# Sorted chunks of a graph layer with 424 edges and one scatter, scatters that wait for picking, and another order within a step

## The chip, the cores and the metric

The kernel runs as one program on one core of a Trainium2 chip. The metric is the device time of one execution in microseconds (us). The engines are named as the profile names them: PE is TensorE (PEld are its weight loads), DVE is VectorE, ACT is ScalarE, POOL is GpSimd and SP is SyncE. Lines such as L947 are lines of the kernel before; the lines of the changed kernel differ.

## The reference, cut to what matters

A message-passing layer over 412,500 edges that are sorted by `dst`, with 12,500 nodes of 128 features:

```python
h = jnp.maximum(_layernorm(x, axis=-1), 0.0)
# of the layer, with idx_i = src (not sorted) and idx_j = dst (sorted):
h = h @ W_in2f
Wij = ssp(f_ij @ W_f1 + b_f1) @ W_f2 + b_f2     # ssp(x) = softplus(x) - log 2; f_ij: 20 numbers an edge
Wij = Wij * rcut_ij[:, None]
x_ij = h[idx_j] * Wij                           # the message of an edge
agg = jax.ops.segment_sum(x_ij, idx_i, num_segments=N)
out = ssp(agg @ W_o1 + b_o1) @ W_o2 + b_o2
x = x + out
```

Two parts are irregular: `h[idx_j]` is read by an index that is sorted, and the messages are summed by an index that is not.

## The kernel before

Edges are taken in chunks of 512 (four tiles of 128), four chunks are a group, and there are 204 groups, of which 814 chunks hold edges. `step(k)` writes out one step of a software pipeline in which every engine does its share for another chunk; the order of the calls in it is the order of the instructions on each engine, since the schedule is written by hand. In step k:

- `rows` (SP, six chunks ahead) loads the 32 rows of `h` that a chunk can need into `near`; they are kept as three bfloat16 parts. `window` (DVE) makes `at`, which marks the row of each edge, and `pick` (PE, two chunks ahead) multiplies the two, which gives `h[idx_j]` for each edge in `ps`. `picked` (ACT) scales it by `rcut_ij`.
- `hidden` (PE), `exp` and `log` (ACT) make ssp(f W_f1 + b) for two chunks at a time in the one bank `z`; `value` (PE, one chunk ahead) multiplies it by W_f2 onto the bias that `bias` (ACT) has put into `v`.
- `message` (DVE) multiplies the two into `o`, a buffer of two chunks; there are four such buffers.
- Then POOL scatters `o` into a table in DRAM, one indirect DMA for each tile of 128 edges: edge by edge to `slot`, a row that belongs to the node block (128 nodes) of its `src`. The table is written through 16 views (`VIEWS`), which the kernel declares to be disjoint, in turn. A scatter waits until the scatter that last used its semaphore (eight before) or its view has landed.
- `blocks`, `rank` and `rank_end` (DVE and PE) find `slot`: a running count for each of the 98 node blocks is kept in one bank of PSUM, `free`, and `top` is read from it.

A segment (`SEGS`, eight runs of groups) has a table of its own. After a segment its table is read back and summed by node: `load` (SP) brings tiles of 128 slots (`m`), `compare` (DVE) marks the node of each slot (`to`), `add` (PE) multiplies the two into `acc`, a tile being one matmul of two passes, and `keep` (DVE) adds four blocks to `agg`. A planner spreads these units over the later steps; from the sizes of the segments it gives 6.08 tiles a step from step 245, and 8.86 from step 629 to the end of the edges. The last segment's 206 tiles come after the last scatter, with the output layers between them.

In 32 groups (`SORTED`, from group 6 to 150, four or five groups apart) the edges of a chunk are first sorted by node block. `Permute` does it on the chip, 19 to 4 steps ahead; its `move` multiplies the edges' data by marks into `z` and `moved` (ACT) copies `z` to `ev`. A chunk then has only 480 edges (`PV` of each 128), laid out so that 256 (`FIXED`) stand at fixed places. Those tiles are stored by a plain DMA into `fix` (the list `statics`, issued in the next step), and only the other two tiles of the chunk need a scatter. `ev` holds the marks in its last 32 partitions, so `Permuted.pick` takes three matmuls of 32 rows for each tile, one for each part of `h`.

Of the kernel before, what the change touches and what calls it, by code (L numbers as in the profile page):

```python
# [23 lines left out]
SEGS = (59,39,30,27,19,14,8,8)  # L24
RW = P + 1
VIEWS = 16
# [11 lines left out]
PV = 120  # L38
# [3 lines left out]
FIXED = 2 * P  # L42
# [23 lines left out]
def gnn_kernel(  # L66
# [31 lines left out]
    assert D == P and src_n.shape == (P, NT) and NW <= P  # L98
# [14 lines left out]
    class Segment:  # L113
# [4 lines left out]
        def __init__(self, k):  # L118
# [10 lines left out]
            self.kw = NW if here and here[-1] == permuted[-1] else 0  # L129
# [19 lines left out]
            self.rows = self.row(NBLK)  # L149
            self.all = self.rows + self.nw * FIXED  # L150
# [25 lines left out]
        def row(self, b):  # L176
            return (b * self.T + min(max(b - self.b0, 0), self.b1 - self.b0)) * P
# [57 lines left out]
    fix = tc.dram_tile([NW * FIXED, RW], F32, name="fix")  # L235
# [138 lines left out]
    def permute_constants():  # L374
# [29 lines left out]
        for T in sels:  # L404
            edge_t = T * P
            half_t = edge_t / 2
            for t, (e0, e1, c) in enumerate(((1.0, 0.0, -edge_t), (0.5, 0.5, -half_t - 1.0),
                                             (0.5, 0.5, -half_t), (0.0, 1.0, -1.0))):
                turn_t = -1.0 if t % 2 else 1.0
                nc.vector.memset(lifts[T][:, t:t + 1], c - BIG * turn_t)  # L410
# [251 lines left out]
    with tc.tile_pool(name="edge", bufs=2) as edge, tc.tile_pool(  # L662
# [47 lines left out]

        class Group:


            def __init__(self, g):
# [30 lines left out]
                self.near = {}  # L745

            def rows(self, c):
# [8 lines left out]
                nc.sync.dma_start(self.near[c], h3_t[t][bass.ds(start, WR), :]  # L756
                                  .rearrange("r (k f) -> (r k) f", f=P))

            def columns(self):
                if len(self.cols) == 3:  # L760
# [24 lines left out]
                    nc.vector.tensor_copy(start_t[:, :, 0], row_t[:, 0, :, 0])  # L785
                    nc.vector.tensor_add(start_t[:, :, 1:3], row_t[:, 0, :, 1:3],
                                         row_t[:, 1, :, 1:3])
                    for t, half in ((1, -1.0), (2, 0.0)):
                        nc.vector.tensor_scalar(start_t[:, :, t], start_t[:, :, t], 0.5,
                                                seg.T * P / 2 + half, op0=ALU.mult, op1=ALU.add)  # L790
                    nc.vector.tensor_scalar(start_t[:, :, 3], row_t[:, 1, :, 3],
                                            seg.T * P - 1.0, None, op0=ALU.add)
# [55 lines left out]
            def rank_end(self, c):  # L848
# [63 lines left out]
            def value(self, c, v):  # L912

                r = self.pair[c // 2 * 2][:, c % 2, :]
                for i in range(QT):
                    nc.tensor.matmul(v[:, i, :], r[:, i * P:(i + 1) * P], wf2,  # L916
                                     start=False, stop=True, skip_group_check=True)
                return v

            def pick(self, c, at, ps):  # L920

                near = self.near.pop(c)
                for i in range(QT):
                    nc.tensor.matmul(ps[:, i, :], at[:, i * P:(i + 1) * P], near,  # L924
                                     start=i == 0, stop=i == QT - 1, skip_group_check=True)

# [9 lines left out]
            def message(self, c, v, hg):  # L936
# [6 lines left out]
                nc.vector.tensor_mul(o[:, :, :P], v, hg)  # L943
                views = self.seg.views
                for i in range(QT):
# [6 lines left out]
                    )  # L952
                    due = [self.seg.clears[w] for w, d in enumerate(self.seg.cleared)
# [14 lines left out]
        class Permuted(Group):  # L968


            def __init__(self, g):
                super().__init__(g)
                self.from_ = permutes[g]

            def rows(self, c):

                k = self.g * NCHUNK + c
                t = table_of[k]
                i = int(k >= FIRST)
                at = k - heads[i].start  # L980
                if c % 2 == 0:
                    self.near_p = quad_room().bitcast(BF16)
                self.near[c] = self.near_p[3 * WR:, c % 2 * 3 * P:(c % 2 + 1) * 3 * P]
                start = nc.sync.value_load(shifts[i][0:1, at:at + 1], min_val=0,
                                           max_val=tables[t][1] - WR)
                nc.sync.dma_start(self.near[c], h3_t[t][bass.ds(start, WR), :])
# [14 lines left out]
            def over(self, c, i):  # L1001

                s = self.from_.scalars.rearrange("p (w t) i -> p w t i", w=NCHUNK)
                return s[:, 2 * c:2 * c + 2, 0:2, i]

            def blocks(self, c):
                if c < NCHUNK - 1:
                    return
                for h in range(2):
                    blk = edge.tile([P, QT], F32, name="blk_p")  # L1010
                    nc.vector.tensor_scalar(blk.rearrange("p (w t) -> p w t", w=2),
                                            self.over(h, 2), -1.0, None, op0=ALU.add)
                    inb = quad.tile([P, QT, NBLK], F16, name="inb", bufs=4)
                    nc.vector.tensor_tensor(
                        inb, count_ps[:, None, :NBLK].to_broadcast([P, QT, NBLK]),
                        blk[:, :, None].to_broadcast([P, QT, NBLK]), op=ALU.is_equal)
                    self.inb[h] = inb.rearrange("p t b -> p (t b)")

            def rank(self, c):

                if c < 2:
                    return
                self.pass_on()
                kept["inb"] = self.inb[c - 2]
# [3 lines left out]
            def rank_end(self, c):  # L1028

                if c < 2:  # L1030
                    return
                h = c - 2
# [4 lines left out]
                top_w = top.rearrange("p (w t) -> p w t", w=2)  # L1037
                nc.vector.tensor_add(top_w, top_w, self.over(h, 3))
# [831 lines left out]
```

## Time and profile before

| | us |
|---|---|
| three runs | 3958.76, 3964.23, 3968.8 |
| median | 3964.23 |
| the profiled execution | 3958.62 |
| its span, first to last instruction | 3956.9 |

| engine | busy us | share of the span | instructions |
|---|---|---|---|
| PE | 3331.5 | 84% | 24536 |
| PEld | 2657.4 | 67% | 24536 |
| DVE | 3116.8 | 79% | 8634 |
| ACT | 2437.4 | 62% | 5637 |
| POOL | 2896.1 | 73% | 3018 |

TensorE's granted clock was 0.91 of full speed on average. In a group's row, the numbers after the bar are its busy time in us and the mean of one instruction in ns, and after the second bar the idle time of the engine just before them with what ended most of it; "issue" is time in which the profile shows nothing that the engine waited for. A row of waits has the total in us, the number of waits and the longest. In the timeline a row has the start, the length, and in brackets the idle time before it and its releaser.

### The profile page before, as it was taken

Reading aid. Unit: us, or ns where it says so; the run is one execution under the profiler, and the core shown is the slowest. Engines: PE = TensorE matmul, PEld = TensorE weight load, DVE = VectorE, ACT = ScalarE, POOL = GpSimd, SP = SyncE. Lnnn points to the kernel's source line nnn. Section 1 sums busy time; section 2 is a strip of 40 time slices with the busy share of each in tenths; the row PEclk is TensorE's granted clock in tenths of the full one; section 3 lists DMA queues with packets and bytes.
Section 4 is the critical chain, followed back from the end, with each engine's and each line's share of the span. In section 5 each row is a group of like instructions: output and inputs, shape, how many; then the busy total and the mean of one; then the engine's idle time right before and its main releaser. Section 6 shows DMA issues by size and latency. Waiting matters only on the chain. (4 is left out here: it accounts for less than half of the span.)

```text
span 3956.9 us, 80101 instructions
## 1 busy us (share of the span) xinstructions
PE 3331.5 (84%) x24536; PEld 2657.4 (67%) x24536; DVE 3116.8 (79%) x8634; ACT 2437.4 (62%) x5637; POOL 2896.1 (73%) x3018
## 2 busy tenths in 40 slices
PE   6777877777788988989989989888888889988968
PEld 4555555554467777777767767777676778777867
DVE  7978777766678888888888879788777778787867
ACT  5776677766666666666656656666555555554625
POOL 5777777777777777777777777777777777777760
PEclk9888788887899999999999999999889999999989
DMA  6787666665567878877777767887788779777766
GB/s 171 217 264 246 182 185 177 180 188 167 151 190 222 230 220 253 252 223 219 221 246 231 209 190 206 237 252 205 227 245 235 205 228 288 226 211 216 217 191 189
DMA packets 644371, 852.03 MB, mean 215 GB/s; under 512 B 240230, under 2 KB 442082, under 8 KB 643934
## 3 DMA queue, kind: packets, MB, share of 16 engines
q1 hardware_dynamic: 547502, 648.36, 59.3%
q0 software_dynamic: 96000, 198.34, 15.0%
q8 instruction: 198, 3.24, 0.4%
q14 instruction: 239, 1.96, 0.2%
q10 hardware_dynamic: 432, 0.13, 0.0%
HBM read 427.81 MB, written 418.61 MB: 214 GB/s over the span
## 5 line engine op out<-in xcount | busy, mean ns | idle before, releaser
L947 POOL DMA_INDIRECT slots<-o,slot x2744 | 2646.2, 964 | 868.2 <-issue 642.7
L1378 PEld LDWEIGHTS acc<-to,m 128*128 128x128 f32 x8464 | 1080.7, 205 | 398.2 <-DVE to L1362 171.7
L1378 PE MATMUL acc<-to,m 128*128 128x128 f32 x8464 | 1171.2, 294 | 189.7 <-DVE to L1362 99.2
L916 PEld LDWEIGHTS v<-wf,r 128*128 128x128 f32 x6512 | 916.2, 209 | 125.0 <-ACT v L909 58.6
L916 PE MATMUL v<-wf,r 128*128 128x128 f32 x6512 | 947.8, 293 | 33.2 <-ACT v L909 32.3
L809 ACT ACTIVATE r<-z,bf 128x1024 f32<-128x1024 f32 x407 | 451.7, 1110 | 629.1 <-PE z L801 524.2
L909 ACT ACTIVATE v<-bf 128x512 f32<-128x512 f32 x812 | 488.3, 601 | 545.5 <-DVE o L943 483.5
L932 ACT ACTIVATE hg<-picked,rcut 128x128 f32<-128x128 f32 x2744 | 775.1, 368 | 77.5 <-PE picked L924 77.1
L1362 DVE TENSOR_TENSOR to<-count_ps,m 128x640 f32<-128x640 f16 (+5 forms) x945 | 675.2, 741 | 57.2 <-DMA m<-slots 43.3
L943 DVE TENSOR_TENSOR o<-v,hg 128x512 f32<-128x512 f32 x686 | 468.9, 684 | 65.3 <-ACT hg L932 33.2
L814 ACT ACTIVATE r<-r,half 128x1024 f32<-128x1024 f32 x407 | 462.4, 1136 | 0.0
L924 PE MATMUL picked<-near,at 96*128 96x128 bf16 x2744 | 282.4, 228 | 187.1 <-DVE o L943 98.0
L849 DVE TENSOR_REDUCE top<-free 128x4 f32<-128x392 f32 x686 | 379.4, 553 | 71.3 <-PE free L844 70.4
L801 PE MATMUL z<-f,wf 20*128 20x512 f32 x1372 | 414.8, 682 | 0.0
L818 DVE TENSOR_TENSOR inb<-count_ps,blk 128x392 f16<-128x392 f16 x686 | 380.3, 555 | 38.0 <-PE count_ps L1213 26.1
L924 PEld LDWEIGHTS <-at 96*128 96x128 bf16 x2744 | 225.1, 103 | 220.3 <-issue 188.7
L877 PE MATMUL free<-inb,rest_of 128*128 128x392 f16 x750 | 266.2, 355 | 79.4 <-DVE top L849 77.8
L1087 POOL DMA_INDIRECT slots<-o,slot_p x256 | 247.2, 965 | 78.1 <-issue 47.3
L941 DVE COPY o<-place 128x8 f32<-128x8 f32 x343 | 64.7, 188 | 302.6 <-DMA slots<-o,slot 283.1
L844 PE MATMUL free<-inb,after 128*128 128x392 f16 x686 | 244.6, 356 | 8.6 <-DVE used L883 6.2
L896 DVE TENSOR_SCALAR at<-rel,prow 96x512 bf16<-96x512 bf16 x686 | 246.0, 359 | 0.0
L1074 ACT ACTIVATE hg<-picked,scalars 128x128 f32<-128x128 f32 x512 | 144.4, 367 | 8.5 <-PE picked L1063 8.5
(228 smaller groups left out, 2853.8 us busy)
## 6 DMA issues: line engine op xcount, KB each, us to landing
m<-slots SPq DMA_DIRECT2D x200, 387.0 KB
rel<-rel_d SPq DMA_DIRECT2D x172, 384.0 KB
m<-slots SPq DMA_DIRECT2D x198, 322.5 KB
m<-slots SPq DMA_DIRECT2D x227, 258.0 KB
slots<-zero SPq DMA_DIRECT2D x106, 516.0 KB
m<-slots SPq DMA_DIRECT2D x98, 451.5 KB
slots<-o,slot POOLq DMA_INDIRECT x2744
f<-in_f_n SPq DMA_DIRECT2D x408, 80.0 KB
```

The source lines that it names most:

```text
L801: nc.tensor.matmul(z[:, k, :], wf1[rows, :], self.f[rows, :], start=True, stop=True)
L809: nc.scalar.activation(r, z, AF.Exp, bias=bf1, accum_out=exps[:, i:i + 1])
L814: nc.scalar.activation(r, r, AF.Ln, bias=half, scale=0.5)
L818: nc.vector.tensor_tensor(inb, count_ps[:, None, :NBLK].to_broadcast([P, QT, NBLK]), self.blk[:, c * QT:(c + 1) * QT, None].to_broadcast([ ...
L909: nc.scalar.activation(v, spread(bf2, QT), AF.Copy)
L916: nc.tensor.matmul(v[:, i, :], r[:, i * P:(i + 1) * P], wf2, start=False, stop=True, skip_group_check=True)
L924: nc.tensor.matmul(ps[:, i, :], at[:, i * P:(i + 1) * P], near, start=i == 0, stop=i == QT - 1, skip_group_check=True)
L932: nc.scalar.activation(hg[:, i, :], ps[:, i, :], AF.Copy, scale=self.rcut[:, j:j + 1])
L943: nc.vector.tensor_mul(o[:, :, :P], v, hg)
L947: put = nc.gpsimd.indirect_dma_start(out=views[j % VIEWS], out_offset=bass.IndirectOffsetOnAxis(ap=self.slot[:, j:j + 1], axis=0), in_=o[: ...
L1362: nc.vector.tensor_tensor(to[:p, a:e, :], count_ps[:p, None, :].to_broadcast([p, e - a, P]), self.m[u][:p, a:e, P:].to_broadcast([p, e - a ...
L1378: nc.tensor.matmul(self.acc[b // self.size][:, i, :], m[:p, j, :P], to[:p, j, :], start=t == 0, stop=t == self.seg.read(b) - 1)
```

## The change

Sorted chunks have 424 edges (`PV` 106), `FIXED` is three tiles of four, and the last tile is the only one that is scattered. The same 32 groups are sorted, so that there are three more plain groups: 207 groups, 828 chunks with edges. The four scattered tiles of a sorted group are ranked together, once. The marks of a sorted chunk are copied by DMA to 96 partitions and `near` is loaded in three parts, so that its pick is the plain one, four matmuls of 96 rows. There are seven segments; the planner now gives 4.52 tiles a step from step 257, 6.53 from 481 and 9.54 from 621. Slots are no longer clamped to the table: the start of every block is moved up by half a tile, and the bound on the count is folded into the instruction that turns it.

Within a step the scatters move out of `message` into `put`, behind the picking; `window` stands ahead of the picking; `exp`, the sorting's `moved` and `product` and the ranking follow it; `hidden`, `keep` and `add` come last. The first scatter of each chunk k also waits for the pick of chunk k+2 (`PACE`).

```diff
-SEGS = (59,39,30,27,19,14,8,8)
+SEGS = (62,56,35,24,14,8,8)
+PACE = {0: (("pick", 2),)}
...
-PV = 120
+PV = 106
...
-FIXED = 2 * P
+SETS = (32,)
+FIXED = 3 * P
...
-            self.rows = self.row(NBLK)
-            self.all = self.rows + self.nw * FIXED
+            self.rows = self.row(NBLK) + P // 2
+            self.all = self.rows + self.nw * P
...
+        behind_of = {}
+        def behind(put, name):
+            tc.add_manual_dep(put.ins, name,
+                              mybir.DependencyInfo(mybir.DependencyClass.Sync,
+                                                   mybir.DependencyReason.DATA),
+                              reason="order of scatters")
+        def paced(put, k, i, n):
+            for event, ahead in PACE.get(i, ()) if n > 1 or i else PACE.get(1, PACE.get(0, ())):
+                name = behind_of.get((event, min(k + ahead, NCH - 1)))
+                if name:
+                    behind(put, name)
...
-                    nc.vector.scalar_tensor_tensor(top, top, -BIG,
+                    nc.vector.scalar_tensor_tensor(top, top, BIG + (seg.T + 1) * P / 2 - 1.0,
                                                    turn.rearrange("p c t -> p (c t)")[:, w],
-                                                   op0=ALU.add, op1=ALU.mult)
-                    nc.vector.tensor_add(top, top, self.start[:, w])
-                    nc.vector.tensor_scalar(self.slot[:, w], top, 0.0, float(seg.rows - 1),
-                                            op0=ALU.max, op1=ALU.min)
+                                                   op0=ALU.min, op1=ALU.mult)
+                    nc.vector.tensor_add(self.slot[:, w], top, self.start[:, w])
...
         class Permuted(Group):
...
             def rows(self, c):
                 if c % 2 == 0:
-                    self.near_p = quad_room().bitcast(BF16)
+                    at = quad_room().bitcast(BF16).rearrange("p (w e) -> p w e", w=2)
+                    self.at_of[c // 2] = at
+                    for q in range(WP // WR):
+                        nc.sync.dma_start(at[q * WR:(q + 1) * WR], self.from_.ev[c // 2][WP:])
+                super().rows(c)
...
-            def pick(self, c, at, ps):
-                for i in range(QT):
-                    for q in range(3):
-                        nc.tensor.matmul(ps[:, i, :], at[:, i * P:(i + 1) * P],
-                                         near[:, q * P:(q + 1) * P],
...
-                for i in range(2):
-                    j = c % 2 * 2 + i
-                    nc.gpsimd.indirect_dma_start(
-                        out=self.seg.views[(c * QT + i) % VIEWS],
...
+            def put(self, c):
+                o = self.out.pop(c)
+                put = nc.gpsimd.indirect_dma_start(
+                    out=self.seg.views[c * QT % VIEWS],
+                    out_offset=bass.IndirectOffsetOnAxis(ap=self.slots[:, c:c + 1], axis=0),
+                    in_=o[:, 0, :],
+                    in_offset=None,
+                )
+                paced(put, self.g * NCHUNK + c, 0, 1)
...
         def step(k, units=(), aside=()):
...
-            sorting(k, "moved")
             part("log", min(k + LZ - 2, made["exp"]), pairs(hidden_log))
-            part("exp", min(k + LZ - 1, made["hidden"]), pairs(hidden_exp))
             if has(k):
                 g.message(c, vs.pop(k), hgs.pop(k))
...
+            part("window", k + 3, window)
...
                 g.pick(c, ats.pop(k + 2), ps[k + 2])
...
-            part("window", k + 3, window)
+            if has(k):
+                g, c = of(k)
+                g.put(c)
             for c, u in units:
                 c.compare(u)
                 compared.append((c, u))
-            for c in owed:
-                c.keep()
-            owed.clear()
+            part("exp", min(k + LZ - 1, made["hidden"]), pairs(hidden_exp))
+            sorting(k, "moved")
+            sorting(k, "product")
             if not aside:
                 sorting(k, "taken")
-            part("hidden", k + LZ, pairs(hidden))
-            sorting(k, "product")
-            for c, u in compared:
-                c.add(u)
-            compared.clear()
...
             sorting(k, "ready")
+            part("hidden", k + LZ, pairs(hidden))
             for c, u in units:
                 c.load(u + AHEAD)
+            for c in owed:
+                c.keep()
+            owed.clear()
+            for c, u in compared:
+                c.add(u)
+            compared.clear()
```

What moved shows on three engines. First GpSimd, where a sorted group meets the plain group behind it; `slot_p` marks the scatters of sorted chunks, and the names in brackets are the semaphores that a scatter waits for (DMASW0 to 7 are those of the eight scatters before it). Before:

```order
L1087 DMA slots_118<-o,slot_p 141824x129 [waits DMASW4_49,DVE_49]
L1087 DMA slots_118<-o,slot_p 141824x129 [waits DMASW5_49]
L1087 DMA slots_118<-o,slot_p 141824x129 [waits DMASW6_49,DVE_49]
L1087 DMA slots_118<-o,slot_p 141824x129 [waits DMASW7_49]
L947 DMA slots_118<-o,slot 141824x129 [waits DMASW0_49,DVE_49]
L947 DMA slots_118<-o,slot 141824x129 [waits DMASW1_49]
```

And after the change:

```order
L1106 DMA slots_118<-o,slot_p 136320x129 [waits DMASW4_49,DVE_49,PE_49]
L1106 DMA slots_118<-o,slot_p 136320x129 [waits DMASW5_49,DVE_49,PE_49]
L1106 DMA slots_118<-o,slot_p 136320x129 [waits DMASW6_49,DVE_49,PE_49]
L1106 DMA slots_118<-o,slot_p 136320x129 [waits DMASW0_49,DMASW7_49,DVE_49,PE_49]
L983 DMA slots_118<-o,slot 136320x129 [waits DMASW4_49,DVE_49,PE_49]
L983 DMA slots_118<-o,slot 136320x129 [waits DMASW1_49]
```

The group has four scatters for eight, each with a wait for PE, and the first plain scatter behind it waits for DMASW4, the semaphore of the scatter four before it, instead of DMASW0.

Next TensorE, from the last picking matmul of one step to the value of the next (chunk 378 is picked; `free` is the ranking, `acc` the sums, `z` the hidden layer). Before:

```order
L924 MATMUL picked<-near,at 128x128
L801 MATMUL z<-f,wf_62 128x512 x2
L1378 MATMUL acc<-to,m 128x128 x10
L877 LDWEIGHTS rest_of
L877 MATMUL free<-inb,rest_of 128x392
L844 LDWEIGHTS after
L844 MATMUL free<-inb,after 128x392
L916 MATMUL v<-wf_63,r 128x128 x4
```

And after the change:

```order
L954 MATMUL picked<-near,at 128x128
L906 LDWEIGHTS rest_of
L906 MATMUL free<-inb,rest_of 128x392
L875 LDWEIGHTS after
L875 MATMUL free<-inb,after 128x392
L832 MATMUL z<-f,wf_62 128x512 x2
L1397 MATMUL acc<-to,m 128x128 x5
L945 MATMUL v<-wf_63,r 128x128 x4
```

The sums and the hidden layer moved behind the ranking, to the end of the step, and in this step one unit of sums stands where there were two.

Last ScalarE, near the same place (`hg` is picked, `v` the bias, `r,exps` the exp, `r<-r` the log, `xo<-z` the sorting's copy). Before:

```order
L909 ACTIVATE v<-bf_68 128x512
L809 ACTIVATE r,exps<-z,bf_66 128x1024
L932 ACTIVATE hg<-picked,rcut 128x128 x4
L909 ACTIVATE v<-bf_68 128x512
L1279 ACTIVATE xo<-z 128x1024
L814 ACTIVATE r<-r,half 128x1024
```

And after the change:

```order
L963 ACTIVATE hg<-picked,rcut 128x128 x4
L938 ACTIVATE v<-bf_68 128x512
L1298 ACTIVATE xo<-z 128x1024
L963 ACTIVATE hg<-picked,rcut 128x128 x4
L938 ACTIVATE v<-bf_68 128x512
L840 ACTIVATE r,exps<-z,bf_66 128x1024
```

The exp and the sorting's copy moved from the beginning of their steps to the end, behind the bias.

More of the change, by code (lines that the diff above doesn't have):

```diff
@@ L128, in __init__ @@
             self.here = here
-            self.kw = NW if here and here[-1] == permuted[-1] else 0
+            ended = [i for i in range(len(SETS)) if permuted[sum(SETS[:i + 1]) - 1] in here]
+            assert len(ended) < 2 and sum(SETS) == NPG
+            self.set = ended[0] if ended else None
+            self.kw = SETS[self.set] * NCHUNK if ended else 0
             plain = (self.c1 - self.c0 - self.nw) * CH
@@ L745, in __init__ @@
                 self.near = {}
+                self.out = {}
             def rows(self, c):
```

119 lines of the change are left out of this document (56 added, 63 removed).

## The prediction

> **What bounds the kernel now.** I read the page's first part, then its costliest groups, then busy time by stretch, because the engine with the most busy time (TensorE) is not the one that sets the end.
>
> ```profile
> span 3956.9 us, 80101 instructions
> L947 POOL DMA_INDIRECT slots<-o,slot x2744 | 2646.2, 964 | 868.2 <-issue 642.7
> L1087 POOL DMA_INDIRECT slots<-o,slot_p x256 | 247.2, 965 | 78.1 <-issue 47.3
> ```
>
> GpSimd looks 73% busy, but it does nothing except scatter, and before nearly every scatter stands a gap that nothing ends ("issue"). The next rows are GpSimd's timeline at the start and the end, and one line of the waits.
>
> ```profile
> 27.25 1.13 POOL L947 DMA_INDIRECT slots<-o,slot  x1 [23.71 <-DVE at L896]
> 39.70 0.96 POOL L947 DMA_INDIRECT slots<-o,slot  x1 [7.55 <-DVE at L896]
> 40.97 0.95 POOL L947 DMA_INDIRECT slots<-o,slot  x1 [0.30 <-issue]
> 3842.14 0.96 POOL L947 DMA_INDIRECT slots<-o,slot  x1 [0.30 <-issue]
> POOL slots L947 <- issue: 642.7, 2107, 0.3
> L947 POOLq EVENT_SEMAPHORE  x720: 17/17/2349, 39.5 to 3833.0; - x180
> ```
>
> A scatter is 0.964 us and its gap 0.30 us, so one takes 1.265 us of GpSimd, and a plain chunk (four) takes 5.06 us. Busy time by stretch (each row: the stretch and its length, then busy us and count of PE, PEld, DVE, ACT and POOL, TensorE's clock, DMA share, GB/s) shows that the queue never stops: the scatters come to 778, 798, 475 and 790, and 2841 x 1.265 = 3594 of the 3600 us from 200 to 3800.
>
> ```profile
> 200.00:1190.00 990.00, 755.89 (x4918) 527.48 (x4917) 733.40 (x2395) 680.15 (x1596) 752.99 (x778) 0.83 0.66 193
> 1190.00:2200.00 1010.00, 903.97 (x7205) 740.28 (x7205) 847.71 (x2321) 650.48 (x1504) 766.89 (x798) 0.96 0.80 231
> 2200.00:2800.00 600.00, 532.58 (x4147) 436.68 (x4144) 495.22 (x1291) 375.52 (x871) 455.44 (x475) 0.94 0.76 215
> 2800.00:3800.00 1000.00, 872.43 (x6560) 749.56 (x6559) 761.96 (x1784) 551.32 (x1292) 759.35 (x790) 0.92 0.79 228
> ```
>
> So GpSimd's scatter queue is the bound from 40 to 3843 us; 114 us of last sums and output follow. What the rest could do without it shows in the waits of VectorE for a free `o` (four buffers of two chunks, freed by landed scatters). These rows are, in turn, from the first, second, third and fourth of those stretches.
>
> ```profile
> DVE o L941 <- DMA slots<-o,slot: 89.8, 26, 8.6
> DVE o L1081 <- DMA slots<-o,slot: 49.8, 17, 7.2
> DVE o L941 <- DMA slots<-o,slot_p: 4.1, 1, 4.1
> ...
> DVE o L941 <- DMA slots<-o,slot: 35.1, 24, 4.4
> DVE o L1081 <- DMA slots<-o,slot: 33.1, 9, 8.6
> DVE o L941 <- DMA slots<-o,slot_p: 8.3, 5, 3.7
> ...
> DVE o L1081 <- DMA slots<-o,slot: 24.2, 6, 6.8
> DVE o L941 <- DMA slots<-o,slot: 15.9, 7, 5.7
> DVE o L941 <- DMA slots<-o,slot_p: 5.1, 2, 3.2
> ...
> DVE o L941 <- DMA slots<-o,slot: 138.3, 54, 6.4
> ```
>
> The messages (L943 and L1084, one a chunk) count the chunks in the same stretches:
>
> ```profile
> 200.00:1190.00 990.00, 116.85 (x171) 0.83 0.66 193
> 1190.00:2200.00 1010.00, 118.15 (x173) 0.96 0.80 231
> 2200.00:2800.00 600.00, 73.11 (x107) 0.94 0.76 215
> 2800.00:3800.00 1000.00, 136.13 (x199) 0.92 0.79 228
> ...
> 200.00:1190.00 990.00, 34.30 (x50) 0.83 0.66 193
> 1190.00:2200.00 1010.00, 34.23 (x50) 0.96 0.80 231
> 2200.00:2800.00 600.00, 16.43 (x24) 0.94 0.76 215
> ```
>
> That is 221, 223, 131 and 199 chunks; the stretches are cut near chunks 257, 481 and 612, where the change moves sums. Without the waits (143.7, 76.5, 45.2, 138.3 us) a chunk would take the other engines 3.83, 4.19, 4.24 and 4.33 us. This free pace is somewhat flattering, since they work ahead during a wait.
>
> **The scatters removed (the main term).** Plain chunks go from 686 to 700, sorted chunks stay 128 with one scatter for two: 2800 + 128 = 2928 scatters for 3000. 72 x 1.265 = -91.1 us of the queue that sets the end. It holds as long as the queue stays full. GpSimd's need for a chunk becomes (4 x plain + sorted) x 1.265 / chunks: 4.20, 4.21, 4.37 and, where nothing is sorted, 5.06 us. Against the free pace, 0.37, 0.02, 0.13 and 0.73 us a chunk are left over, so the second and third stretch need the smaller terms.
>
> **Sums.** 4164 tiles for 4232, but placed otherwise: the planner's rate from chunk 257 to 481 falls from 6.08 to 4.52 tiles a step, from 481 to 621 it rises to 6.53, after that from 8.86 to 9.54. The rows here are the sums (L1378) in the second stretch, and three groups that the next parts use.
>
> ```profile
> 1190.00:2200.00 1010.00, 370.03 (x2706) 341.89 (x2706) 0.96 0.80 231
> L924 PE MATMUL picked<-near,at 96*128 96x128 bf16 x2744 | 282.4, 228 | 187.1 <-DVE o L943 98.0 <-DVE o L1084 37.7 <-ACT hg L932 28.5
> L1063 PE MATMUL picked<-xo 32*128 32x128 bf16 x1536 | 110.5, 219 | 21.5 <-DVE o L943 9.6 <-DVE o L1084 5.5 <-ACT hg L932 2.8
> L809 ACT ACTIVATE r<-z,bf 128x1024 f32<-128x1024 f32 x407 | 451.7, 1110 | 629.1 <-PE z L801 524.2
> ```
>
> A pass of the sums takes 370.03 / 2706 = 0.137 us of TensorE, a tile two passes, 0.27 us. So TensorE gets 0.43 us a chunk lighter, then 0.12 and 0.19 us heavier.
>
> **Sorted chunks elsewhere.** Picking falls from twelve matmuls of 0.072 us to four of 0.103: -0.45 us a sorted chunk, -0.10 us on average. One ranking for two, and no clamp, make VectorE lighter too. None of this is on GpSimd's path, so it earns nothing by itself, but the free pace becomes 3.73 us (first), 3.66 (to chunk 481), 4.26 (to 612) and 4.52 (rest), against needs of 4.20, 4.21, 4.37 and 5.06. GpSimd stays last everywhere, by 0.11 us where it is closest. Fourteen more chunks cost ScalarE the most, whose 680 of 990 us have room. The stores of sorted rows grow by half (128 x 66 KB more) while less is cleared, at a DMA share of 0.66 to 0.80: 0.
>
> **SyncE.** Its issues go from 3630 to 3995: a sorted group issues twelve small loads of `near` and six copies of its marks where it issued four. A short issue was 0.37 us:
>
> ```profile
> 2026.11 0.37 SPq L1471 DMA_DIRECT2D fix<-o  x1
> 2008.47 0.95 POOL L947 DMA_INDIRECT slots<-o,slot  x1 [0.30 <-issue]
> 2011.36 0.17 DVE L1081 COPY o<-scalars 128x8 f32<-128x8 f32 x1 [1.00 <-DMA slots<-o,slot]
> 2018.57 0.96 POOL L947 DMA_INDIRECT slots<-o,slot  x1 [0.30 <-issue]
> 2025.29 0.18 DVE L1081 COPY o<-scalars 128x8 f32<-128x8 f32 x1 [8.58 <-DMA slots<-o,slot]
> ```
>
> 14 x 0.37 = 5.2 us within four steps of some 17 us, issued six steps ahead of the pick (L1469), which is the cover: 25 us. Zero; if the cover went, up to 5.2 us on each of 32 groups.
>
> **A new wait behind the sorted groups.** Slots are written through sixteen views in turn, and the sorted chunks now use views 0, 4, 8 and 12. In the new order the first scatter after a sorted group waits for the one four before it (view 0 again), where every scatter otherwise waits for the one eight before. Four scatters are 5.06 us. How long a scatter takes to land is told by the last four rows above. The scatter begun at 2008.47 is the last of the buffer that the copy at 2011.36 waited for, 2.9 us; from 2018.57 to 2025.29 it is 6.7 us. So a sorted group costs 0 to 1.7 us on GpSimd's own path, all later scatters standing behind it: 0 to 54 us over 32. I take 0.5 us: the middle of the two landings, 4.8 us, just passes without a wait, so about half of them would pay, up to 1.7 us: +16 us.
>
> **Scatters wait for picking.** Four scatters queue behind each such wait. Wherever VectorE waits for an `o`, GpSimd is some six chunks behind, so picking two chunks on is long past; and one more semaphore to look at is 17 ns (the row above), with the same 0.30 us gap in front of scatters that have one or none: 0, at most 828 x 0.017 = 14 us. At the start GpSimd is not behind; the first chunk's wait disappears in the 7.55 us that it idles anyway, the next few cost: +1 us (-1 to +6).
>
> **The step's new order.** Sums now stand last on TensorE, `exp` behind picking on ScalarE, and sorting's matmuls right behind the pick, needing the bank that `exp` frees. If TensorE waits there, it is for at most one such pass of ScalarE (L809, 1.1 us) at four steps of a sorted group, 4.4 us. The spare in a cycle (18.6 chunks, before chunk 481) is 8 us or more, so nothing; from 481 to 612 it is about 2.3 us, so up to 2.1 us on seven groups, 15 us. ScalarE idles a third of the time and should be ahead: +4 us (0 to 15). The tail works through 206 tiles as before: 0 (4 us either way).
>
> **Sum.** The profiled execution took 3958.6 us (span 3956.9), 5.6 below the median of 3964.2 and the least of the three. 3958.6 - 91.1 + 16 + 1 + 4 = 3888.5, call it 3888.
>
> **A rule weighed.** TensorE's clock was 0.83 in the first stretch at 76% busy and 0.96 in the second at 90%. A chunk took it 903.97 / 223 = 4.05 us; less 0.43 and 0.10, 3.52 of 4.21 us is 84% busy from chunk 257 to 481, in between. At a clock of 0.83 its 3.52 us would be 4.07, and the free pace 4.21: no spare.
> The Trainium skill, "TensorE: Matmul & The Clock Gate", section "Part 1: The HAM clock gate", says the array is throttled by default and only sustained activity frees it; by that rule the lighter sums slow every matmul there. The two clocks agree in direction; the sum would rise as in the first rival.
>
> **Rivals.** *GpSimd runs dry behind sorted groups.* With no spare from 257 to 481, the 4.4 us is paid by twelve groups there too, 53 us at most, and 15 us after: 3905 to 3945. For it: the clock rows. Against: 0.55 us spare at the present clock. 0.17.
> *TensorE's order becomes the bound (slower).* In front of every value stand the sums of the step before, and what fitted beside two scatters of a sorted chunk must now fit beside one. Over the 588 chunks from 24 to 612 GpSimd needs 4.24 us on average. From a pace of 4.40 the 91 us are gone, from 4.42 the run is slower: 0.1 us a chunk is 59 us. At 4.55: 3867.5 + 588 x 0.31 = 4050. The free paces of 3.7 to 4.3 speak against it. 0.08.
> *The change doesn't do it:* the landing wait costs its 54 us and GpSimd runs dry for the rest, 3947 to 3970. 0.07.
> *Better:* landings stay under 5.06 us and nothing runs dry, 3862 to 3870. 0.06.
>
> **Chances and range.** The forecast, 3870 to 3905, gets 0.62. With the first rival up to 3935 and the better case, 3863 to 3935 holds eight in ten. About 0.3% (12 us) is what this kernel's measurement can tell from no change. Faster is 0.62 + 0.17 + 0.06 = 0.85, the same 0.07, slower 0.08.
>
> **What would show it.** 2928 scatters at 0.96 us, gaps of 0.30 us but for one of 0.5 us or so behind each sorted group, put down to a landing; GpSimd still 158 a 200 us; VectorE's waits for `o` halved in the first 2800 us and still there after; TensorE's clock under 0.96 from 1150 to 2150 us. I am wrong if GpSimd shows gaps of several us, or waits for picking in mid-run, or scatters longer than 0.96 us.

## The result, and the profile after

The changed kernel took 3911.8 us (median of runs from 3906.7 to 3918.3) beside 3963.0 us for the kernel before, a ratio of 0.9871 (0.9848 to 0.9893). Measured again with more runs beside the experiments, it took 3906.1 us beside 3959.3: 0.9855 (0.9839 to 0.9870). So it is 51 to 53 us faster. The forecast of 3888 was some 20 us too good, and its range, 3863 to 3935, holds the time. The profiled execution took 3918.3 us, with a span of 3916.6 (40.3 less than before). It is the slowest of its four runs, and the profiled one of before is as fast as the fastest of its own, so the two profiles show some 11 us less than the medians do.

The lines of after that answer to those shown of before are, first, the page's first line and the two groups of scatters (L983 and L1106 were L947 and L1087):

```profile
span 3916.6 us, 78744 instructions
L983 POOL DMA_INDIRECT slots<-o,slot x2800 | 2704.0, 966 | 919.1 <-issue 622.1 <-PE picked L954 54.8 <-DMA slots<-o,slot 38.4
L1106 POOL DMA_INDIRECT slots<-o,slot_p x128 | 124.9, 976 | 46.3 <-issue 18.0 <-PE picked L954 8.2 <-DVE to L1381 3.7
```

There are 2928 scatters for 3000, of nearly the same length (966 for 964 ns). A picking is new among the releasers in front of them. The landing (38.4 us, in waits of 0.3 us at most) stood there before too, with 62.5 us; the long landing waits do not show in these rows, because the profile puts them down to other engines, as will be seen. GpSimd's timeline at the start and the end:

```profile
33.19 1.13 POOL L983 DMA_INDIRECT slots<-o,slot  x1 [29.64 <-PE picked L954]
34.62 0.96 POOL L983 DMA_INDIRECT slots<-o,slot  x1 [0.30 <-issue]
39.73 0.96 POOL L983 DMA_INDIRECT slots<-o,slot  x1 [1.63 <-PE picked L954]
3796.85 0.96 POOL L983 DMA_INDIRECT slots<-o,slot  x1 [0.30 <-issue]
```

The first scatter starts 5.9 us later, since it waits for the picking of chunk 2, but the second chunk's gap shrinks from 7.55 to 1.63 us. The last scatter ends at 3797.8 us, 45.3 earlier; 118.8 us follow it, where it was 113.8. Busy time by stretch, with the same columns as before:

```profile
200.00:1190.00 990.00, 755.12 (x4642) 508.81 (x4643) 737.78 (x2340) 725.76 (x1672) 748.72 (x772) 0.83 0.71 203
1190.00:2200.00 1010.00, 889.25 (x6508) 692.04 (x6507) 797.84 (x2175) 697.99 (x1588) 759.85 (x790) 0.92 0.76 214
2200.00:2800.00 600.00, 536.00 (x4127) 436.80 (x4127) 488.05 (x1223) 383.22 (x871) 438.02 (x453) 0.95 0.83 239
2800.00:3800.00 1000.00, 885.96 (x6792) 747.60 (x6791) 755.88 (x1634) 545.80 (x1234) 757.46 (x789) 0.94 0.80 227
```

At 1.265 us for each, a full queue would do 783, 798, 474 and 791 scatters in these stretches. Three are nearly full; the third lacks 21, some 27 us. VectorE's waits for a free `o` in the first three stretches say how much the others had in hand:

```profile
DVE o L972 <- DMA slots<-o,slot: 29.3, 15, 6.0
DVE o L1097 <- DMA slots<-o,slot: 28.8, 10, 7.7
DVE o L972 <- DMA slots<-o,slot_p: 11.5, 4, 3.9
...
DVE o L1097 <- DMA slots<-o,slot: 27.0, 8, 5.0
DVE o L972 <- DMA slots<-o,slot: 11.1, 7, 2.9
DVE o L972 <- DMA slots<-o,slot_p: 2.3, 2, 1.5
...
DVE o L972 <- DMA slots<-o,slot: 8.3, 6, 2.9
```

They fell from 143.7 to 69.6, from 76.5 to 40.4 and from 45.2 to 8.3 us. In the third stretch next to nothing is left in hand.

Where the queue stands still can be counted scatter by scatter: whatever a gap has over 0.30 us is lost. In all it was 10.8 us before and 46.0 after. The start has 6.5 us less of it. Of the new part, 22.9 us are landing waits in front of 14 of the 32 first scatters behind a sorted group. Another 18.1 us are waits for a picking: 17.2 between 2370 and 2490 us (10.4 of it in front of two of the other first scatters, 6.8 in sorted chunks) and 0.9 in front of a plain chunk at 2331 us. The span then follows from the two profiles: 72 scatters at 1.262 us (the usual time from one start to the next) are -90.9; the start gives -0.6, the landing waits +22.9, the waits for picking +18.1, other gaps +0.7, slightly longer scatters +4.5, the tail +5.0. Together that is the -40.3 measured.

Two places show how such gaps look. The first is GpSimd behind the third sorted group:

```profile
337.17 0.95 POOL L1106 DMA_INDIRECT slots<-o,slot_p  x1 [0.30 <-PE picked L954]
338.43 1.08 POOL L1106 DMA_INDIRECT slots<-o,slot_p  x1 [0.30 <-issue]
339.81 0.95 POOL L1106 DMA_INDIRECT slots<-o,slot_p  x1 [0.30 <-issue]
341.07 0.96 POOL L1106 DMA_INDIRECT slots<-o,slot_p  x1 [0.30 <-PE free L875]
345.17 1.17 POOL L983 DMA_INDIRECT slots<-o,slot  x1 [3.14 <-DVE early_room L1235]
```

The scatter at 345.17 goes through view 0, as did the one at 337.17. VectorE is named for an instruction that ended just ahead, but the message that this scatter needs had ended 12.5 us before, and the landing of the scatter at 337.17 stands in the trace 0.77 us ahead of 345.17, 7.2 us after its issue. In all 14 gaps the start follows that landing by 0.77 to 0.78 us. The second place is in the third stretch:

```profile
2379.19 0.96 POOL L1106 DMA_INDIRECT slots<-o,slot_p  x1 [1.89 <-PE picked L954]
2381.76 0.96 POOL L1106 DMA_INDIRECT slots<-o,slot_p  x1 [1.61 <-PE picked L954]
2385.58 0.96 POOL L1106 DMA_INDIRECT slots<-o,slot_p  x1 [2.87 <-DVE to L1381]
2390.73 0.96 POOL L983 DMA_INDIRECT slots<-o,slot  x1 [4.20 <-DVE top L880]
2391.99 0.96 POOL L983 DMA_INDIRECT slots<-o,slot  x1 [0.30 <-issue]
```

Here the view was free, and in the first four rows, whatever they name, GpSimd started 0.28 us after the end of the picking two chunks on. It had overtaken the others. TensorE's rows ahead of the fourth show what that picking stood behind, the sums of the step before and the value:

```profile
2386.94 2.39 PE L1397 MATMUL acc<-to,m 128*128 128x128 f32 x20
2389.17 1.06 PE L945 MATMUL v<-wf,r 128*128 128x128 f32 x8
2390.07 0.39 PE L954 MATMUL picked<-near,at 96*128 96x128 bf16 x4
```

### The profile page after: what moved, and what is told of

It reads as the page before. It is cut to its first block, busy times and chain, and to the rows that moved or that the text cites. A ratio compares the mean times of both kernels' runs of the same rounds, so it can differ in the third digit from the quotient of the medians.

```text
span 3916.6 us, 78744 instructions
## 1 busy us (share of the span) xinstructions
PE 3309.6 (85%) x23536; PEld 2561.9 (65%) x23536; DVE 3026.4 (77%) x8128; ACT 2530.3 (65%) x5728; POOL 2831.6 (72%) x2946
## 5 line engine op out<-in xcount | busy, mean ns | idle before, releaser
L983 POOL DMA_INDIRECT slots<-o,slot x2800 | 2704.0, 966 | 919.1 <-issue 622.1
L1397 PE MATMUL acc<-to,m 128*128 128x128 f32 x8328 | 1144.9, 294 | 51.0 <-DVE agg L1420 30.9
L963 ACT ACTIVATE hg<-picked,rcut 128x128 f32<-128x128 f32 x2800 | 792.9, 366 | 521.6 <-PE picked L954 482.4
L945 PE MATMUL v<-wf,r 128*128 128x128 f32 x6624 | 970.8, 294 | 30.4 <-ACT v L938 30.2
L945 PEld LDWEIGHTS v<-wf,r 128*128 128x128 f32 x6624 | 893.8, 208 | 153.1 <-ACT v L938 69.1
L1381 DVE TENSOR_TENSOR to<-count_ps,m 128x640 f32<-128x640 f16 (+4 forms) x939 | 670.1, 737 | 105.9 <-DMA m<-slots 85.7
L845 ACT ACTIVATE r<-r,half 128x1024 f32<-128x1024 f32 x414 | 475.3, 1148 | 12.9
L832 PE MATMUL z<-f,wf 20*128 20x512 f32 x1400 | 452.7, 726 | 2.2 <-ACT xo L1298 2.1
L875 PEld LDWEIGHTS <-after 128*128 128x128 f16 x700 | 71.5, 102 | 295.5 <-issue 284.7
L832 PEld LDWEIGHTS z<-f,wf 20*128 20x128 f32 x1400 | 115.0, 200 | 126.0 <-issue 88.9
```

The source lines that it names most:

```text
L832: nc.tensor.matmul(z[:, k, :], wf1[rows, :], self.f[rows, :], start=True, stop=True)
L845: nc.scalar.activation(r, r, AF.Ln, bias=half, scale=0.5)
L945: done = nc.tensor.matmul(v[:, i, :], r[:, i * P:(i + 1) * P], wf2, start=False, stop=True, skip_group_check=True)
L963: nc.scalar.activation(hg[:, i, :], ps[:, i, :], AF.Copy, scale=self.rcut[:, j:j + 1])
L983: put = nc.gpsimd.indirect_dma_start(out=views[j % VIEWS], out_offset=bass.IndirectOffsetOnAxis(ap=self.slot[:, j:j + 1], axis=0), in_=o[: ...
L1381: nc.vector.tensor_tensor(to[:p, a:e, :], count_ps[:p, None, :].to_broadcast([p, e - a, P]), self.m[u][:p, a:e, P:].to_broadcast([p, e - a ...
```

## The experiments

The open questions: whether the landing waits and the waits for picking are what the time is made of, or only where GpSimd happens to wait for something slower; what the dry stretch and the longer tail come from; and whether a scatter really is worth 1.26 us. Eight kernels ran on two chips on which the kernel before took 3959 and 3963 us (a0 to e3 on the first, e4 to e9 on the second), and four on a third chip that turned out to be another case. The dry stretch is chunk 460 to 612, where GpSimd's queue ran empty.

**e1_views: the landing wait taken away.**

```diff
-                    out=self.seg.views[c * QT % VIEWS],
+                    out=self.seg.views[QT + c],
```

> The sorted chunks' scatters go through views 4 to 7 in place of 0, 4, 8 and 12; the first scatter behind the group then finds view 0 last used eight scatters back, as anywhere else. Theory (the wait for a landing four scatters back lies on GpSimd's own path): the 14 landing waits of 22.9 us go, and the time falls by 15 to 23 us, to 3889 to 3897. Rival (there GpSimd only waits for what the other engines set anyway; a landing taken away comes back as waits for messages or picking): less than 6 us, 3906 or more, with the gaps put down to VectorE or TensorE.

**a0_after** is the measure for it and its two companions.

> The changed kernel as it is, the measure for the others: 3912 us, 0.987 of the kernel before. The gaps in front of the first scatter behind a sorted group add up to about 33 us again, in 14 to 18 of the 32 groups.

Measured: a0_after 3906.1 us, with 31.3 us of gaps behind sorted groups at 18 of them; 15 of these, 16.6 us, are landing waits, the others waits for a picking. e1_views 3890.0 us, 0.9820 (0.9807 to 0.9834): 16 us less, at the lower end of what the theory said and far from the rival. It is what a0_after's landing waits come to. GpSimd behind the third sorted group of e1_views:

```profile
337.26 0.96 POOL L1106 DMA_INDIRECT slots<-o,slot_p  x1 [0.30 <-PE picked L954]
338.53 0.96 POOL L983 DMA_INDIRECT slots<-o,slot  x1 [0.30 <-issue]
```

The gap is gone, and so are all landing waits. Behind sorted groups 10.9 us are left at three places, two of them the long waits for picking of 3.9 and 6.5 us. From chunk 24 to 460 the excess falls from 13.7 to 1.5 us: there nothing else took the wait's place.

**e2_no_pace: no scatter waits for a picking.**

```diff
-PACE = {0: (("pick", 2),)}
+PACE = {}
```

> No scatter waits for a picking. Theory (the two long gaps behind sorted groups and those inside sorted chunks, 17.8 us in all, are this wait, and the message was ready 2.5 and 4.7 us sooner): 7 to 14 us faster, 3898 to 3905; at the start the first scatter begins at 27 in place of 33 us, which the next gap takes back. Rival (between chunk 460 and 612 GpSimd is dry because the other engines need more per chunk than it does; without the wait it only runs dry at the next message): within 5 us of the changed kernel.

Measured: 3904.0 us, 0.9858 (0.9842 to 0.9873), 2 us less than a0_after. The rival was right. The first scatter starts at 26.5 us, and the next gap takes 5.6 us back. In the dry stretch GpSimd waits about the same two sorted groups as before, only for the message instead:

```profile
2374.48 0.96 POOL L1106 DMA_INDIRECT slots<-o,slot_p  x1 [1.19 <-DVE at L925]
2378.33 0.96 POOL L983 DMA_INDIRECT slots<-o,slot  x1 [2.89 <-DVE o L974]
2385.26 0.95 POOL L983 DMA_INDIRECT slots<-o,slot  x1 [2.20 <-DVE o L974]
```

Each starts 0.28 us after its chunk's message, and the gaps of the stretch are 22.9 us for 28.3. So most of what the dry stretch costs is there without the wait for picking.

**e3_views_no_pace: both.** The two edits above together.

> Both edits together. If the landing wait and the wait for picking lie on GpSimd's path one behind the other, the gains add: 22 to 37 us, 3875 to 3890. If the other engines' pace from chunk 460 to 612 is what is left, 15 to 20 us of gaps stay there and the time is 3892 to 3900.

Measured: 3880.4 us, 0.9802 (0.9788 to 0.9815), 26 us less than a0_after. That is 8 more than the two apart, about what these intervals leave open; taken away on top of e1, the wait for picking is worth 10 us and not 2, and how much of that is its own stays open. The gaps behind sorted groups fall from 31.3 to 4.2 us. What is left, 8.8 us in the profile, stands between chunk 460 and 612; 118.3 us follow the last scatter.

**e5_one_more: 128 scatters more.** Each sorted chunk issues a second scatter of the same rows, into a table that nothing reads.

```diff
                 paced(put, self.g * NCHUNK + c, 0, 1)
+                nc.gpsimd.indirect_dma_start(
+                    out=spare_rows[c][:, :],
+                    out_offset=bass.IndirectOffsetOnAxis(ap=spare_at[:, 0:1], axis=0),
+                    in_=o[:, 0, :], in_offset=None)
```

> Each sorted chunk issues a second scatter of the same 128 rows, into rows that nothing reads: 128 scatters more. Theory (a scatter is worth its 1.26 us wherever GpSimd's queue is full): 128 x 1.26 = 161 us more, less the 25 to 30 us of landing waits and dry gaps that a longer queue covers: 3912 + 161 - 28 = 4045, within 4030 to 4060. Rival (a part of the scatters taken away was covered by other engines' work): 3990 to 4025.

Measured: 4037.3 us beside 3963.4 for the kernel before, 1.0187 (1.0171 to 1.0203). It is inside the theory's 4030 to 4060. In the two profiles, 128 x 1.262 = 161.5, less 39.5 us of gaps (44.1 in a0_after, 4.6 here), less 3.7 of scatter lengths, and 2.6 of tail make 120.9 of the 120.7 us between the spans. No gap over 0.5 us is left behind chunk 24, so with two scatters for a sorted chunk GpSimd is last everywhere. With one it is not. Since the added scatters write elsewhere, view 0 was here again last used eight scatters before, so the landing waits go for e1's reason.

**e4_old_order: the step's order of before.** The scatters stay behind picking; `exp` and `moved` go back to the start of the step, `keep`, `hidden`, `product` and the sums in front of the ranking.

```diff
+            sorting(k, "moved")
             part("log", min(k + LZ - 2, made["exp"]), pairs(hidden_log))
+            part("exp", min(k + LZ - 1, made["hidden"]), pairs(hidden_exp))
...
-            part("exp", min(k + LZ - 1, made["hidden"]), pairs(hidden_exp))
-            sorting(k, "moved")
-            sorting(k, "product")
+            for c in owed:
+                c.keep()
+            owed.clear()
...
+            part("hidden", k + LZ, pairs(hidden))
+            sorting(k, "product")
+            for c, u in compared:
+                c.add(u)
+            compared.clear()
             for r in tops:
```

> The changed kernel with a step's parts in the order of before (exp and moving the sorted rows at the start, hidden product, sorting's matmuls and the sums in the middle, in front of the ranking), only the scatters still behind picking. Theory (the new order costs a few us between chunk 460 and 612 at most, the need of the engines there is set by the sums): within 10 us of the changed kernel, gaps of 25 to 35 us from chunk 460 to 612 as now. Rival (the new order is what makes the sums late for the messages' engines or early for them): more than 15 us either way, with the gaps from chunk 460 to 612 under 15 or over 45 us.

Measured: 3906.8 us, 0.9857 (0.9842 to 0.9872), the changed kernel's own time. The profile is divided: 11.8 us of gaps between chunk 460 and 612 for 28.3, as the rival had it, but 19.2 for 13.7 ahead of them. And the gaps are of another kind. These rows stand where a0_after waits 6.0 us for a picking:

```profile
2383.04 0.96 POOL L1106 DMA_INDIRECT slots<-o,slot_p  x1 [0.30 <-issue]
2388.85 0.95 POOL L983 DMA_INDIRECT slots<-o,slot  x1 [4.85 <-DVE o L972]
```

The second starts 0.78 us behind the landing of the scatter four before it, as does every scatter of the stretch that waits over 0.5 us longer than usual. No such wait for a picking or a message is left, where a0_after has some 23 us of them; in their place GpSimd waits longer for landings, 28 us in all for 16.6. The time says that the new order as a whole costs and earns nothing that can be measured. What it does to the dry stretch alone stays open, since one profile is too little: a0_after's is the slowest of its four runs and e4's the fastest, and e9 below has the same plan there as e3 and 18.2 us of gaps for 8.8.

**e8_fewer_sums: the sums moved out of the dry stretch.** On e3.

```diff
-SEGS = (62,56,35,24,14,8,8)
+SEGS = (62,56,40,19,14,8,8)
```

> On the kernel with both waits away (3880 us), the third segment takes 40 groups and the fourth 19 in place of 35 and 24, so the planner's rate from chunk 481 on falls from 6.53 to 5.71 tiles a step and rises after that from 9.54 to 10.49. Theory (between chunk 460 and 612 the sums make TensorE and VectorE need more than GpSimd): the 8.8 us of gaps there fall under 3 us, 3872 to 3876 if the last segments' sums still end in time. Rival (the gaps are the sorting's own and stay): 3878 to 3884 with 7 to 10 us of gaps there.

Measured: 3903.2 us, 0.9846 (0.9833 to 0.9859), 17 to 23 us slower than e3, which neither side expected. The mechanism shows all the same. GpSimd's queue is full through the stretch, with 0.5 us of gaps for 8.8 between chunk 460 and 612 (for 18.2 in e9 on the same chip), and the last scatter ends at 3752.5 for 3757.8:

```profile
2349.61 0.96 POOL L983 DMA_INDIRECT slots<-o,slot  x1 [0.30 <-issue]
2350.87 0.96 POOL L983 DMA_INDIRECT slots<-o,slot  x1 [0.30 <-issue]
2352.13 0.95 POOL L1106 DMA_INDIRECT slots<-o,slot_p  x1 [0.31 <-DVE top L880]
...
3751.53 0.95 POOL L983 DMA_INDIRECT slots<-o,slot  x1 [0.31 <-issue]
```

But 145.9 us follow it for 118.3. The sums of the earlier segments end 40.5 us behind the last scatter for 9.6, because the steps did not get the 10.49 tiles that were planned: in the order of TensorE's instructions 402 tiles stand behind the last picking for 322. That the engines were too slow for them the profile doesn't show: GpSimd's gaps behind chunk 612 are 0.9 us, as in e3. The likely reason is the plan itself, which takes at most two units in a step and leaves the rest to the end. So with this order the gaps go when the sums get fewer, and the sums that are moved away are paid at the end.

**e9_sums_sooner: the planner's end.** On e3.

```diff
-        end = NCH + 6
+        end = NCH + 1
```

> On the same kernel (3880 us) the planner ends the earlier segments' sums at step NCH + 1 in place of NCH + 6, which lifts the last rate from 9.54 to 9.77 tiles a step. Theory (the output waits for sums that now end some 10 us behind the last scatter; 4 us before the change): the stretch behind the last scatter falls from 118 to 112 to 114 us, the time to 3875. Rival (that stretch starts with the last scatter's landing and the loads of the last segment, whatever the sums do): no change within 2 us.

Measured: 3887.8 us, 0.9809 (0.9796 to 0.9823), not to be told from e3. The tail did what the theory says, and more: 107.5 us for 118.3. The queue in front of it ended 16.7 us later, 9.4 of it in the dry stretch, whose plan is that of e3, and most of the rest in scatters that took longer; both figures come from one profile of each kernel. What links the tail to the sums is VectorE's timeline behind the last scatter, of before, of after and of e9_sums_sooner: the last sum of the earlier segments (`agg`) and the first compare of the last segment (`to`).

```profile
3847.28 0.42 DVE L1401 TENSOR_TENSOR agg<-agg,acc 128x256 f32<-128x256 f32 x1 [0.65 <-PE acc L1378]
3853.85 2.46 DVE L1362 TENSOR_TENSOR to<-count_ps,m 128x768 f32<-128x768 f16 x4
...
3807.94 0.42 DVE L1420 TENSOR_TENSOR agg<-agg,acc 128x256 f32<-128x256 f32 x1 [0.65 <-PE acc L1397]
3813.91 2.47 DVE L1381 TENSOR_TENSOR to<-count_ps,m 128x768 f32<-128x768 f16 x4
...
3779.01 1.29 DVE L1381 TENSOR_TENSOR to<-count_ps,m 128x768 f32<-128x768 f16 x2 [6.67 <-DMA m<-slots]
```

Before and after, the compare follows that sum by 6.6 and 6.0 us; from the last scatter it is 10.8 and 16.1 us. In e9 it waits for its own load and comes 4.6 us behind the last scatter. So the late sums were worth their 5 us behind the last scatter, and the last segment's landing is the floor under them; the whole run did not get faster.

**The last four kernels ran on a chip on which the bound is another.** There the kernel before took 5241 us, at a TensorE clock of 0.80 (0.91 on the other two).

e11_even_sums is e3 with `SEGS = (54,36,36,27,24,14,8,8)`:

> On the kernel with both waits away (3880 us; 8.8 us of gaps from chunk 460 to 612, 118 us behind the last scatter): segments of 54, 36, 36, 27, 24, 14, 8 and 8 groups, 4270 tiles for 4164. The planner's rates are 5.30 tiles a step to chunk 513, 5.67 to 621 and 9.04 after that, in place of 4.52, 6.53 and 9.54. Theory (sums placed too densely cost twice, as gaps from chunk 460 to 612 and as sums behind the last scatter): gaps there under 3 us and 108 to 114 us behind the last scatter, 3862 to 3870. Rival (the 106 tiles more and the eighth segment cost as much): 3876 to 3884.

e12_even_sooner is that with `end = NCH + 1`:

> The same, with the earlier segments' sums planned to end at step NCH + 1 (last rate 9.26). Theory (each step sooner takes up to 2 us off the stretch behind the last scatter while the rate stays under 9.5): 104 to 110 us behind the last scatter, 3856 to 3866, not above the run without it. Rival (what ends the tail is the last segment's landing and loads): within 2 us of the run without it.

e13_after_even is the changed kernel with these segments alone:

> The changed kernel with only these segments; both waits stay. Theory: the gaps from chunk 460 to 612 fall from 28 to 8 to 14 us (what is left are landing waits), the tail by 5 us or more, 3882 to 3890; the landing waits of the other stretches stay at 12 to 16 us. Rival (those gaps are the two waits', not the sums'): 3900 to 3908.

e10_order_again is e3 with the order of e4:

> The kernel with both waits away (3880 us) and the step's parts in the order of before, where no landing wait blurs the count. Theory (the new order costs nothing that the sums' rate does not cost already): gaps from chunk 460 to 612 of 5 to 18 us as with the new order, 3874 to 3888. Rival (the new order costs 10 to 16 us there): gaps under 4 us, 3866 to 3872.

Measured, as ratios to the kernel before on that chip: e11 0.9835 (0.9804 to 0.9866), e12 0.9862 (0.9833 to 0.9890), e13 0.9215 (0.9188 to 0.9242), e10 1.0001 (0.9979 to 1.0023). None of the expectations came true or can be judged, because GpSimd's queue is not the bound there. Busy time from 500 to 1100 us, of e3 on the first chip, then of e13 and e11:

```profile
500.00:1100.00 600.00, 456.13 (x2793) 298.70 (x2793) 432.61 (x1394) 440.16 (x1011) 456.06 (x473) 0.82 0.64 180
...
500.00:1100.00 600.00, 406.72 (x2256) 268.20 (x2255) 372.36 (x1204) 364.72 (x837) 363.68 (x376) 0.76 0.56 158
...
500.00:1100.00 600.00, 394.53 (x2122) 263.02 (x2123) 344.84 (x1125) 340.32 (x781) 338.63 (x350) 0.71 0.53 150
```

GpSimd did 376 and 350 scatters where a full queue does 474. So the question of e11 to e13, whether an even plan of the sums would earn both the dry stretch and the tail, wasn't answered, nor was e10's.

## Why the prediction was right, and where it was off

*GpSimd's queue is the bound, and 72 scatters are worth 91 us.* Right. The queue is nearly full in three stretches of four, and e5 shows the same price from the other side, 128 scatters more for 161.5 us less the gaps that they fill. That the scatters got some 4.5 us longer in all was not foreseen, and its cause is open.

*A new wait behind the sorted groups, +16 us.* Right in place and mechanism, a little small. "About half of them would pay" came true, 14 of 32, but the mean wait was 1.64 us and not 1.0. The step that was short is the bound: a wait begins not when a landing takes longer than the 5.06 us between the two scatters but at 4.28, since the scatter starts 0.78 us behind the landing; and landings reached 7.2 us where the two rows gave 6.7. Taken away, it earned 16 us alone and 24 on top of e2. That the sum came near is partly luck: "half of them" was read off two landings.

*Scatters wait for picking, 0, and +1 at the start.* The start came out at -0.6. In mid-run the trace shows 18.1 us of waits for picking, with gaps of up to 6.8 us, which I had named as signs that I was wrong. For the most part it was the dry stretch instead: e2 took the wait away and 2 us came back (10 on top of e1, at the edge of what the intervals can tell).

*The step's new order, +4 us from chunk 481 to 612.* This is the term that was mis-sized: 18.1 us of waits for picking, and the stretch lacks 27 us with its landing waits in it. The spare of 0.11 us a chunk was right as "closest", and the stretch was the one named, but I let the sorted groups pay there only a wait behind `exp`. e8 shows that the cost hangs on the 6.53 tiles a step: at 5.71 nothing is left of it. My reading of why, which no run isolates: a mean over the stretch hid that a sorted chunk needs 1.26 us of GpSimd but as much of the other engines as a plain one, so GpSimd runs up to them within each group, and a spare of 2.3 us in a cycle does not refill what it has used. But it may hang on the order as well: in e4's profile the old order, at the same 6.53 tiles, has no such wait left. In e4's time that doesn't show, so the order's share stays open.

*The tail, 0.* It cost 5 us. I compared the number of tiles of the last segment, 206 before and after, and not when the segments ahead of it end: their last rate went up from 8.86 to 9.54 tiles a step, their sums ended 10.1 us behind the last scatter instead of 4.2, and the last segment's compares follow them by 6 us.

*The rivals.* The first said GpSimd would run dry from chunk 257 to 481 too, by way of a slower TensorE. The clock did fall in the second stretch, from 0.96 to 0.92, with TensorE busy 88% of it for 90%. The rule of the Trainium skill, "TensorE: Matmul & The Clock Gate", section "Part 1: The HAM clock gate", agrees in direction. The price did not come: from chunk 257 to 460 the gaps were 8.6 us, nearly all landing waits, and 40.4 us of waits for `o` were left. Its other half, the 15 us for chunks 481 to 612, is what happened in place and size. *TensorE's order becomes the bound* did not come for the run as a whole: outside the dry stretch the queue stayed full on the first two chips, but for landing waits.

## What to carry to other kernels

Where a queue is the bound, count its items for the main term, and for what remains look at the stretch with the smallest spare, within one cycle of the pattern and not on its mean: an engine that gets lighter only for a few items in a row catches up with the others there, and then shows every wait they have. A wait for a resource used n items ago holds from n periods less the time from the event to the start (0.78 us here), so widen the reuse distance before shortening a queue. Work that is moved out of a tight stretch must be given room where it goes: e8 won 8 us of gaps and lost 28 behind the last scatter.

## What was not expected of the hardware

The time from a scatter's issue to its landing runs from 2.3 to 6.6 us (5% to 95%), with a median of 4.3 (after) to 4.4 (before), and a scatter that waits for a landing starts 0.77 to 0.78 us after it (0.75 in e2, without the wait for PE).

The chips differ. The same kernel before took 3959, 3963 and 5241 us on three of them. On the third a scatter (962 ns), a DMA packet of one (median 160 ns) and VectorE's multiply (686 for 684 ns) were as long as elsewhere, while a matmul of the sums took 318 ns on average for 292, and what TensorE made came late. ScalarE's waits in e11 on that chip and in e3 on the first:

```profile
ACT hg L963 <- remote: 576.5, 130, 10.1
ACT hg L963 <- PE acc L1397: 200.8, 47, 7.5
ACT hg L963 <- PE picked L954: 165.3, 84, 6.0
...
ACT hg L963 <- PE picked L954: 471.9, 299, 6.5
```

"Remote" is a releaser that the profile could not place. Where ScalarE stood idle over 0.15 us before it scaled a chunk's picked rows, it started 0.04 us behind that picking's end in the trace in e3 (median of 347), and 2.9 us in e11 (median of 459, 7.8 at 95%). TensorE's ends are modelled, so perhaps the model is too early there. On that chip the kernel that keeps both waits (e13) was 6% faster than the one without them (e11), against the sign on the first chip (a0_after and e3). Why stays open; the two kernels differ in nothing but the views and the wait for picking.
